# Causal windowed attention times a gated binary FFN: the products with v ahead of the scores in each step of the attention, k of the first sequence projected by halves, its v in PSUM of the attention

## The chip, the core and the metric

One Trainium2 chip, of which one core runs the kernel. The metric is the device time in microseconds (us); the median of three runs counts. A profile is taken of one execution of its own, whose time is given beside its span, the stretch that the records of the engines cover. Short names of the engines: PE is TensorE, DVE VectorE, ACT ScalarE, POOL GpSimd, SP SyncE (it issues DMAs). PEld is the loading of weights on PE.

## The reference

Eight sequences of 512 tokens with 256 channels. The normalised input goes into an attention of 16 heads of 16 channels with rotary positions, in which a token sees itself and the 249 before it, and into a network of three layers whose weights are +1 or -1; the attention's output times silu of the network's is added to the input.

```python
# x: [8, 512, 256]
xn = layernorm(x)
q, k, v = split(xn @ in_proj_w.T)          # 16 heads x 16
q, k = rotate(q), rotate(k)
mask = (delta >= 0) & (delta < 250)        # delta = pos_q - pos_k
attn = softmax(where(mask, q @ k.T / 4, lowest))
s = concat_heads(attn @ v) @ out_proj_w.T
h = s0 * (concat(xn, -xn) @ sign(k0))      # 512 -> 1024
h = s1 * (2 * relu(h) @ sign(k1))          # 1024 -> 1024
h = s2 * (2 * relu(h) @ sign(k2))          # 1024 -> 256
y = x + s * silu(h)
```

## The kernel before

**The order of work.** The body is a list of pieces, each with a place on an axis of planned time, a cost and a function. `run` (L226) sorts them by place and calls them one after another; its clock is the sum of the costs. A function issues its matmuls and may return followers, each with a delay; a follower is put out before the first piece at which the clock has passed its time. Each engine executes what it was given in this order, and waits for buffers and data by semaphores. So the places in `everything` (L966), in `prepare` (L446) and in `attention` (L827), and the delays, are the whole schedule. A sequence takes 42 units (`SEQ`, L213).

**What a sequence does.** For the first sequence x is transposed on PE (`turn_x`, L315); its parts for the network (a high part in fp16, a low part in fp32r) come from `first_parts` (L349), which is called for tiles 0 and 1 from the list and for 2 and 3 behind the last transpose. For the others the statistics go through DRAM and are applied to a transposed load (`stats` L245, `lay_down`, `lay_over`, `norm_turned`). `project` (L368) makes the parts a and b of k and of q, each in two matmuls of 128x512, multiplies them by cosine and sine on DVE (`times`), rotates on POOL (`rotate`), splits into high and low on ACT and DVE (`split_hi`, `split_lo`), writes both to DRAM and loads them stacked by groups of four heads (`stack`, L438). `project_v` (L354) makes v in four tiles of 128 tokens, which ACT copies into `v_pad`. The network's layers are in `layer` (L481): matmuls of the high, then of the low parts, a relu on ACT that writes the high part, and a subtraction on DVE that writes the low one. The third layer is `last` (L533).

**Attention.** A sequence's attention has nine steps (L682), spread over its 42 units between matmuls of the network. In a step (L819) `scores` (L701) issues the scores of up to 512 columns for four heads into two PSUM tiles; `exponentials` (L723) has ACT write them to p in two halves and POOL set to zero what the mask excludes (`mask`, L740); `values` (L767) multiplies p of the step before with v into `po`. A step thus issues its own scores, then the products of the step before (`flush`, L812), and hands out the exponentials of its own as followers. When a group's last products are issued, `keep` (L797) takes po out of PSUM: numerators V and sums S. S is inverted on DVE (`invert`, L861), V multiplied on POOL (`divide`, L865), and `project_o` (L887) projects and adds x.

**PSUM.** Three pools: `ps_s` two tiles of two banks (the two halves of a step's scores; at the start also two of the transposes and q of the first sequence), `ps_o` one tile (`po`, and the target of the warm-up matmuls, `warm`, L220), `ps_m` three tiles of one bank, which serve all else: h, v, k, q, z, the output's projection. A function that takes a tile waits until its last user has read it.

**The start.** Nine warm-up matmuls, two transposes, two more warm-ups, two transposes, one more warm-up, then k, q, the first layer with a tile of v after the second, fourth, sixth and eighth of its groups, and the second layer. Between them ACT and POOL make the weights of the second layer from bytes (`make_w1`, L188). A fallback for inputs with vanishing variance or huge scores (L1000 on) is compiled and doesn't run.

```python
0819  def step(b, i):
0820      sc, n = scores(b, i)
0821      had = len(pending)
0822      more = flush() or []
0823      p, masks, exps = exponentials(b, i, sc, n)
0824      pending.append((exps, masks, (b, i, p)))
0825      return [(-0.7 if had else 0.0, exps)] + more
```

Of the kernel before, what the change touches and what calls it, by code (L numbers as in the profile page):

```python
# [11 lines left out]
F32 = mybir.dt.float32  # L12
# [22 lines left out]
def tile_attention_times_gated_ffn(  # L35
# [42 lines left out]
    nc = tc.nc  # L78
    P = 128
    B, T, E = x.shape  # L80
    H = HEADS
# [233 lines left out]
    def turn_x(b, t, plain=False):  # L315

        st = states[b]
        xn = xs.pop((b, t))
        if t == 0:
            st["xT"] = one.tile([P, EC, T], F32, tag="xT", name=f"xT_{b}")  # L320
            if plain:
                st["xp"] = one.tile([P, EC, T], F32, tag="xl", name=f"xp_{b}")
            else:
                for p, dt in (("h", F16), ("l", F32R)):
                    st["x" + p] = one.tile([P, EC, T], dt, tag="x" + p, name=f"x{p}_{b}")
        if not plain and t < 2:

            pt = ps_s.tile([P, 2, T], F32, tag="sc", name=f"xnT_ps_{b}_{t}")
            pt = pt[:, 0, : EC * P].rearrange("p (c q) -> p c q", c=EC)
        else:  # L330
            pt = ps_m.tile([P, EC, P], F32, tag="mm", name=f"xnT_ps_{b}_{t}")
        for c in range(EC):
            nc.tensor.transpose(pt[:, c, :], xn[:, ts(c, P)], ident)
        if plain:
            nc.vector.tensor_copy(st["xT"][:, :, ts(t, P)], pt)
            nc.scalar.mul(st["xp"][:, :, ts(t, P)], pt, sgnx)
            return
        hi, lo = (st["x" + p][:, :, ts(t, P)] for p in "hl")


        nc.scalar.copy(st["xT"][:, :, ts(t, P)], pt)
        st["parts", t] = [
            lambda: nc.scalar.mul(hi, pt, sgnx),
            lambda: nc.vector.scalar_tensor_tensor(lo, pt, sgnx, hi, ALU.mult, ALU.subtract),
        ]
        if t + 1 == NT:
            first_parts(2, 3)

    def first_parts(*tiles):  # L349
        for t in tiles:  # L350
# [2 lines left out]

    def project_v(b, t):  # L354
        st = states[b]
        v = ps_m.tile([P, H // 2, 2, D], F32, tag="mm", name=f"v_ps_{b}_{t}")
        for c in range(EC):
            nc.tensor.matmul(  # L358
                v.rearrange("p n s d -> p (n s d)"),
                st["xT"][:, c, ts(t, P)],  # L360
                wqkv_sb[:, c, 2 * E :],
                start=(c == 0),
                stop=(c == EC - 1),
            )
        return [(0.0, lambda: nc.scalar.copy(v_pad[:, t, :, 0:3:2, :], v))]  # L365


    def project(b, what, part):  # L368
        st = states[b]
        col = E * "qk".index(what) + P * "ab".index(part)  # L370
        if b == 0 and what == "q":
            ps = ps_s.tile([P, 2, T], F32, tag="sc", name=f"{what}{part}_ps_{b}")[:, 0]
        else:
            ps = ps_m.tile([P, T], F32, tag="mm", name=f"{what}{part}_ps_{b}")
        for c in range(EC):
            nc.tensor.matmul(  # L376
                ps, wqkv_sb[:, c, ds(col, P)], st["xT"][:, c, :],
                start=(c == 0), stop=(c == EC - 1),
            )

        m = turned.tile(
            [P, 2, T], F32, tag=f"m{part}", name=f"m_{what}{part}_{b}",
# [1 line left out]
        )  # L384
        st[what, part] = m

        hi_after, lo_after = (4.0, 5.1) if b else (7, 8.2) if what == "k" else (6, 7.2)

        def times(i):
            nc.vector.tensor_tensor(  # L390
# [55 lines left out]
    def prepare(b, plain=False):  # L446

        if b == 0 or plain:
            at = dict(stats=-40, norm=-38, x=-36, k=0, q=3, v=9.2)
            dp, dv = 1.5, 1.5  # L450
        else:

            at = dict(load=9, stats=9, down=10.5, over=12, norm=16.8, k=21.8, q=24.8, v=SEQ + 0.6)
            if b == 1:
                at.update(load=18.65, stats=12, down=18.64, over=19.5, norm=23, k=27, q=29)
            dp, dv = 1.5, 1.0
            at = {n: SEQ * (b - 1) + f for n, f in at.items()}
        out = [(at["stats"], 0, lambda: stats(b))]
# [12 lines left out]
                ]  # L471
            out.append((at["v"] + dv * t, 0.87, lambda t=t: project_v(b, t)))
        for what in "kq":
            out += [
                (at[what], 1.75, lambda w=what: project(b, w, "a")),
                (at[what] + dp, 1.75, lambda w=what: project(b, w, "b")),
            ]
        return out


# [336 lines left out]
            return values(*of_step)  # L817

    def step(b, i):  # L819
        sc, n = scores(b, i)  # L820
        had = len(pending)
        more = flush() or []
        p, masks, exps = exponentials(b, i, sc, n)
        pending.append((exps, masks, (b, i, p)))
        return [(-0.7 if had else 0.0, exps)] + more

    def attention(b, among):  # L827
# [17 lines left out]
        for g in range(NG):  # L845

            at = times[used[g - 2][-1]] + 0.01 if g > 1 else first - (
                2.0 if b == 0 else 4.0 if b == 1 else 9.0
            )
            if b and g == 1:  # L850
                at = first + 0.01
# [3 lines left out]
        return out  # L855

    def ends_at(b):
        return SEQ * b + (30.0 if b + 1 == B else SEQ)


    def invert(b, pair, n):  # L861
# [76 lines left out]
    def divisions(b):  # L938
        out = []
        for pair in range(2):  # L940
            if b + 1 < B:
                first, d = (SEQ * b + 30.0, 2.0) if pair == 0 else (SEQ * (b + 1) + 4.2, 2.0)
            else:
                first, d = SEQ * b + (20.0 if pair == 0 else 30.6), 1.3
            for n in range(4):
                out.append((first + d * n, 0, lambda p=pair, n=n: invert(b, p, n)))
            out.append((first + d * 4, 0, lambda p=pair: divide(b, p)))
# [13 lines left out]
    def swap():  # L961
# [2 lines left out]
        outs = ctx.enter_context(tc.tile_pool(name="outs", bufs=1))  # L964

    everything = [  # L966
        (-34.6, 0, signs), (-40.5, 0, lambda: warm(9)), (-34.7, 0, lambda: warm(2)),
        (-32.5, 0, lambda: warm(1)), (-31.0, 0, lambda: enough(0)),
        (-32.7, 0, lambda: first_parts(0, 1)),
        (19.2, 0, make_w2), (22.5, 0, swap), (SEQ * (B - 1) + 45.0, 0, add_up),  # L970
    ]
    for c in range(EC):
        everything += [
# [153 lines left out]
```

## Time and profile before

| | us |
|---|---|
| runs (median of three) | 617.72 (617.2 to 617.77) |
| profiled execution | 617.83 |
| its span | 616.1 |
| PE busy | 598.1 |
| PE loading weights | 367.5 |
| DVE busy | 381.7 |
| POOL busy | 308.8 |
| ACT busy | 294.9 |

Mean granted clock of PE 0.995. By groups of the page, the network's matmuls (h_ps, L497) take 146.5 + 123.1 + 52.3 + 38.4, the products (L786) 77.3, the scores (L712) 57.5, z (L551) 35.8 and v (L358) 33.1 of PE's time. ACT spends 138.3 on 144 halves of exponentials; POOL 91.6 and 48.8 on masks, 722 and 509 ns each.

How to read the lines below. A line of the timeline has start, duration, engine, line and operation, output <- inputs, shape, the number of instructions joined, and in brackets the idle time before it with the engine, tile and line that ended it. PE's time busy is modelled, so a start-to-start difference tells the length of a block better than the durations. A line of the table of stretches has the stretch, its length, busy time and number of instructions of PE, PEld, DVE, ACT and POOL, the granted clock, the DMA engines' busy share and GB/s.

### The profile page before, as it was taken

The numbers are of one execution on the slowest core, as the hardware profiler recorded it, in microseconds if no ns is written. First come the engines' busy times: TensorE is split into PE (matmuls) and PEld (weight loads), VectorE is DVE, ScalarE is ACT, GpSimd is POOL, SyncE is SP. The second block draws the span as 40 slices with busy tenths as digits, with TensorE's granted clock in tenths as the row PEclk, the third lists the DMA queues.
The fourth block names the chain that finished last, engine by engine and source line by source line (L and its number), as shares of the span: only waits on it lengthen the run. The fifth ranks groups of instructions, "written<-read, shape, count | busy, mean of one in ns | idle before, by whom it ended". The sixth has DMA issues, their size and how long they took to land.

```text
span 616.1 us, 11176 instructions
## 1 busy us (share of the span) xinstructions
PE 598.1 (97%) x4490; PEld 367.5 (60%) x4490; DVE 381.7 (62%) x606; ACT 294.9 (48%) x414; POOL 308.8 (50%) x368
## 2 busy tenths in 40 slices
PE   8898999999999999999999999999999999999995
PEld 5453556556655566655565565655565556666794
DVE  7824545665765666655846658566576566655574
ACT  4555465345444355435455454544545435644421
POOL 2943551436723465236654466254672356626642
PEclk9998999999999999999999999999999999999998
DMA  8361370325342163222533153333524216212201
GB/s 275 152 239 53 120 271 20 112 113 194 95 138 89 70 230 113 87 86 109 199 103 121 51 203 106 111 119 115 195 87 141 91 70 224 85 52 70 81 8 40
DMA packets 38061, 74.51 MB, mean 121 GB/s; under 512 B 5360, under 2 KB 13040, under 8 KB 38000
## 3 DMA queue, kind: packets, MB, share of 16 engines
q1 hardware_dynamic: 35568, 71.48, 33.5%
q10 hardware_dynamic: 2432, 2.23, 1.1%
q8 instruction: 37, 0.61, 0.4%
q14 instruction: 24, 0.20, 0.1%
HBM read 44.30 MB, written 29.39 MB: 120 GB/s over the span
## 4 chain that ended last, share of the span: by engine, by line
PE 91%; DVE 4%; POOL 2%; DMA 1%; ACT 1%; issue 1%; SPq 0%; DVEq 0%; ACTq 0%; POOLq 0%
PE h_ps L497 44%; PE po L786 11%; PE z_ps L551 9%; PE sc L712 8%; PE v_ps L358 4%; PE att_ps L895 4%; PE ka_ps L376 3%; PE qb_ps L376 2%; PE qa_ps L376 2%; PE kb_ps L376 2%; PE warm L224 1%; DMA of_all<-d 1%; ACT p L731 1%; DMA d<-moments 1%; DVE den L568 1%
## 5 line engine op out<-in xcount | busy, mean ns | idle before, releaser
L731 ACT ACTIVATE p<-sc 128x1024 f32<-128x1024 f32 (+2 forms) x144 | 138.3, 1013 | 77.9 <-PE sc L712 43.8
L747 POOL TENSOR_SCALAR_AFFINE_SELECT p<-p 128x512 f32<-128x512 f32 x128 | 91.6, 722 | 136.2 <-ACT p L731 135.7
L497 PE MATMUL h_ps<-h1l,w1l_sb 128*128 128x512 f32 (+1 forms) x576 | 146.5, 396 | 0.0
L497 PE MATMUL h_ps<-h1h,w1h_sb 128*128 128x512 f16 (+1 forms) x576 | 123.1, 357 | 0.5 <-ACT v_pad L365 0.5
L497 PEld LDWEIGHTS h_ps<-h1l,w1l_sb 128*128 128x128 f32 x576 | 100.3, 188 | 29.6 <-issue 9.3
L508 ACT ACTIVATE h2h<-h_ps 128x512 f16<-128x512 f32 (+1 forms) x72 | 39.5, 548 | 115.8 <-PE h_ps L497 115.5
L497 PEld LDWEIGHTS <-w1h_sb 128*128 128x128 f16 x576 | 51.2, 98 | 59.0 <-issue 17.8
L754 POOL TENSOR_SCALAR_AFFINE_SELECT p<-p 128x512 f32<-128x512 f32 (+1 forms) x96 | 48.8, 509 | 74.6 <-ACT p L731 72.3
L786 PE MATMUL po<-p,v_pad 128*32 128x378 f32 (+4 forms) x1216 | 77.3, 373 | 3.1 <-DVE S L810 1.2
L612 DVE RECIPROCAL den<-den 128x256 f32<-128x256 f32 (+1 forms) x32 | 52.6, 1645 | 25.2 <-POOL den L607 25.2
L712 PEld LDWEIGHTS sc<-q,k 32*128 32x128 f32 x1216 | 44.1, 184 | 31.9 <-issue 20.6
L506 DVE SCALAR_TENSOR_TENSOR h2l<-h_ps,h2h 128x512 fp32r<-128x512 f32 (+1 forms) x72 | 43.9, 610 | 30.6 <-ACT h2h L508 30.5
L712 PE MATMUL sc<-q,k 32*128 32x378 f32 (+4 forms) x1216 | 57.5, 306 | 2.2 <-ACT p L731 2.2
L506 DVE SCALAR_TENSOR_TENSOR h1l<-h_ps,h1h 128x512 fp32r<-128x512 f32 x64 | 42.7, 679 | 24.7 <-ACT h1h L508 24.7
L863 DVE RECIPROCAL S<-S 128x128 f32<-128x128 f32 x64 | 57.4, 918 | 0.0
L497 PE MATMUL h_ps<-xl,w0l_sb 128*128 128x512 f32 x128 | 52.3, 489 | 0.0
L786 PEld LDWEIGHTS po<-p,v_pad 128*32 128x32 f32 x1216 | 31.7, 109 | 32.0 <-issue 17.7
L508 ACT ACTIVATE h1h<-h_ps 128x512 f16<-128x512 f32 x64 | 38.1, 598 | 21.5 <-PE h_ps L497 21.4
L301 DVE TENSOR_TENSOR xT<-xT,of_all 128x512 f32<-128x512 f32 x28 | 22.5, 805 | 32.2 <-DMA of_all<-d 31.8
L497 PE MATMUL h_ps<-xh,w0h_sb 128*128 128x512 f16 x128 | 38.4, 381 | 0.2 <-ACT v_pad L365 0.2
L551 PE MATMUL z_ps<-h2l,w2l_sb 128*128 128x512 f32 (+1 forms) x144 | 35.8, 390 | 0.0
L358 PE MATMUL v_ps<-wqkv_sb,xT 128*128 128x256 f32 x128 | 33.1, 381 | 2.0 <-DVE h1l L506 2.0
(101 smaller groups left out, 723.5 us busy)
## 6 DMA issues: line engine op xcount, KB each, us to landing
q<-dq SPq DMA_DIRECT2D x64, 256.0 KB, 3.5
dq<-qh SPq DMA_DIRECT2D x16, 512.0 KB, 3.3
dq<-m_qa SPq DMA_DIRECT2D x16, 512.0 KB, 5.3
k<-dk SPq DMA_DIRECT2D x32, 256.0 KB, 2.8
dk<-kh SPq DMA_DIRECT2D x8, 512.0 KB, 3.5
dk<-m_ka SPq DMA_DIRECT2D x8, 512.0 KB, 2.6
x<-in_x_dram SPq DMA_DIRECT2D x30, 128.0 KB, 2.8
xT<-in_x_t_dram SPq DMA_DIRECT2D x7, 512.0 KB, 5.2
```

Of the source, the lines that this page charges most:

```text
L358: nc.tensor.matmul(v.rearrange("p n s d -> p (n s d)"), st["xT"][:, c, ts(t, P)], wqkv_sb[:, c, 2 * E :], start=(c == 0), stop=(c == EC - 1),)
L376: nc.tensor.matmul(ps, wqkv_sb[:, c, ds(col, P)], st["xT"][:, c, :], start=(c == 0), stop=(c == EC - 1),)
L497: nc.tensor.matmul(ph, w[p][:, c, ts(f, P)], st[src + p][:, c, cols], start=(k == 0), stop=(k == n - 1),)
L506: nc.vector.scalar_tensor_tensor(lo, ph, 0.0, hi, ALU.max, ALU.subtract)
L508: high = lambda: nc.scalar.activation(hi, ph, AF.Relu)
L551: nc.tensor.matmul(pz, w2[p][:, c, ts(f, P)], st["h2" + p][:, c, cols], start=(c == 0 and p == "h"), stop=(c == NF1 - 1 and p == "l"),)
L612: nc.vector.reciprocal(part, part)
L712: nc.tensor.matmul(sc[r // 2][:, r % 2, ds(off, n)], st["k0", g][row, ts(j, P)], st[f"q{turn}", g][row, ds(j * P + first, n)], start=(turn ...
L731: nc.scalar.activation(p[:, 2 * half : 2 * half + 2, :n], sc[half][:, :, :n], AF.Exp, scale=D ** -0.5,)
L747: nc.gpsimd.affine_select(out=block, in_=block, compare_op=ALU.is_ge, fill=0.0, base=0, pattern=[[0, 4], [1, P]], channel_multiplier=-1,)
L786: nc.tensor.matmul(po[32 * r : 32 * r + 32, ds(j * P + first, n)], v_columns(j, g, r), p_[:, r, ds(off, n)], start=(j == 0), stop=(done an ...
L863: nc.vector.reciprocal(part, part)
```

## The change

- `step`: the products of the step before are issued first, the step's scores behind them. The exponentials still follow the scores.
- `project` gets `half`: of the first sequence's k, part a and part b, the first 256 columns are projected between and behind the transposes, the other 256 at the old place. The half's PSUM tile is kept until then. Three warm-up matmuls go (`warm(2)` and `warm(1)`; `warm(0)` issues none but still takes the tile).
- `turn_x`: the third transpose goes to `ps_o`, since the half of k takes a tile of `ps_m`. `first_parts` for tiles 0 and 1 comes behind the last transpose and for 2 and 3 from the list.
- `project_v`: v of the first sequence goes to `ps_s`.
- Delays and places: the splits of the first sequence's k and q sooner (4.5 and 5.7, 5 and 6.2, for 7 and 8.2, 6 and 7.2); the second sequence's statistics later and its load, k and q by some tenths of a unit; the first stacked loads 1.5 units sooner; the last sequence's steps over 33 units for 30, its divisions 2.5 and 3 later, the adding up of the counts 2.6 later.

```diff
--- before.py
+++ after.py
@@ -323,7 +323,10 @@
             else:
                 for p, dt in (("h", F16), ("l", F32R)):
                     st["x" + p] = one.tile([P, EC, T], dt, tag="x" + p, name=f"x{p}_{b}")
-        if not plain and t < 2:
+        if not plain and t == 2:
+            pt = ps_o.tile([P, T], F32, tag="po", name=f"xnT_ps_{b}_{t}")
+            pt = pt[:, : EC * P].rearrange("p (c q) -> p c q", c=EC)
+        elif not plain and t < 2:
 
             pt = ps_s.tile([P, 2, T], F32, tag="sc", name=f"xnT_ps_{b}_{t}")
             pt = pt[:, 0, : EC * P].rearrange("p (c q) -> p c q", c=EC)
@@ -344,7 +347,7 @@
             lambda: nc.vector.scalar_tensor_tensor(lo, pt, sgnx, hi, ALU.mult, ALU.subtract),
         ]
         if t + 1 == NT:
-            first_parts(2, 3)
+            first_parts(0, 1)
 
     def first_parts(*tiles):
         for t in tiles:
@@ -353,7 +356,11 @@
 
     def project_v(b, t):
         st = states[b]
-        v = ps_m.tile([P, H // 2, 2, D], F32, tag="mm", name=f"v_ps_{b}_{t}")
+        if b == 0:
+            v = ps_s.tile([P, 2, T], F32, tag="sc", name=f"v_ps_{b}_{t}")[:, 0, :E]
+            v = v.rearrange("p (n s d) -> p n s d", s=2, d=D)
+        else:
+            v = ps_m.tile([P, H // 2, 2, D], F32, tag="mm", name=f"v_ps_{b}_{t}")
         for c in range(EC):
             nc.tensor.matmul(
                 v.rearrange("p n s d -> p (n s d)"),
@@ -365,18 +372,25 @@
         return [(0.0, lambda: nc.scalar.copy(v_pad[:, t, :, 0:3:2, :], v))]
 
 
-    def project(b, what, part):
+    def project(b, what, part, half=None):
+
         st = states[b]
         col = E * "qk".index(what) + P * "ab".index(part)
         if b == 0 and what == "q":
             ps = ps_s.tile([P, 2, T], F32, tag="sc", name=f"{what}{part}_ps_{b}")[:, 0]
+        elif half == 1:
+            ps = st.pop(part)
         else:
             ps = ps_m.tile([P, T], F32, tag="mm", name=f"{what}{part}_ps_{b}")
-        for c in range(EC):
-            nc.tensor.matmul(
-                ps, wqkv_sb[:, c, ds(col, P)], st["xT"][:, c, :],
-                start=(c == 0), stop=(c == EC - 1),
-            )
+            st[part] = ps
+        for cols in [slice(0, T)] if half is None else [ts(half, T // 2)]:
+            for c in range(EC):
+                nc.tensor.matmul(
+                    ps[:, cols], wqkv_sb[:, c, ds(col, P)], st["xT"][:, c, cols],
+                    start=(c == 0), stop=(c == EC - 1),
+                )
+        if half == 0:
+            return
 
         m = turned.tile(
             [P, 2, T], F32, tag=f"m{part}", name=f"m_{what}{part}_{b}",
@@ -384,7 +398,7 @@
         )
         st[what, part] = m
 
-        hi_after, lo_after = (4.0, 5.1) if b else (7, 8.2) if what == "k" else (6, 7.2)
+        hi_after, lo_after = (4.0, 5.1) if b else (4.5, 5.7) if what == "k" else (5, 6.2)
 
         def times(i):
             nc.vector.tensor_tensor(
@@ -452,7 +466,7 @@
 
             at = dict(load=9, stats=9, down=10.5, over=12, norm=16.8, k=21.8, q=24.8, v=SEQ + 0.6)
             if b == 1:
-                at.update(load=18.65, stats=12, down=18.64, over=19.5, norm=23, k=27, q=29)
+                at.update(load=18.65, stats=15, down=18, over=18.7, norm=24.8, k=26.6, q=28.4)
             dp, dv = 1.5, 1.0
             at = {n: SEQ * (b - 1) + f for n, f in at.items()}
         out = [(at["stats"], 0, lambda: stats(b))]
@@ -471,10 +485,17 @@
                 ]
             out.append((at["v"] + dv * t, 0.87, lambda t=t: project_v(b, t)))
         for what in "kq":
-            out += [
-                (at[what], 1.75, lambda w=what: project(b, w, "a")),
-                (at[what] + dp, 1.75, lambda w=what: project(b, w, "b")),
-            ]
+            for n, part in enumerate("ab"):
+                if b == 0 and what == "k" and not plain:
+
+                    out += [
+                        (-34.3 if n == 0 else -32.95, 0.87, lambda p=part: project(b, "k", p, 0)),
+                        (at["k"] + dp * n, 0.87, lambda p=part: project(b, "k", p, 1)),
+                    ]
+                else:
+                    out.append((
+                        at[what] + dp * n, 1.75, lambda w=what, p=part: project(b, w, p),
+                    ))
         return out
 
 
@@ -817,9 +838,10 @@
             return values(*of_step)
 
     def step(b, i):
-        sc, n = scores(b, i)
+
         had = len(pending)
         more = flush() or []
+        sc, n = scores(b, i)
         p, masks, exps = exponentials(b, i, sc, n)
         pending.append((exps, masks, (b, i, p)))
         return [(-0.7 if had else 0.0, exps)] + more
@@ -845,7 +867,7 @@
         for g in range(NG):
 
             at = times[used[g - 2][-1]] + 0.01 if g > 1 else first - (
-                2.0 if b == 0 else 4.0 if b == 1 else 9.0
+                3.5 if b == 0 else 4.0 if b == 1 else 9.0
             )
             if b and g == 1:
                 at = first + 0.01
@@ -855,7 +877,7 @@
         return out
 
     def ends_at(b):
-        return SEQ * b + (30.0 if b + 1 == B else SEQ)
+        return SEQ * b + (33.0 if b + 1 == B else SEQ)
 
 
     def invert(b, pair, n):
@@ -941,7 +963,7 @@
             if b + 1 < B:
                 first, d = (SEQ * b + 30.0, 2.0) if pair == 0 else (SEQ * (b + 1) + 4.2, 2.0)
             else:
-                first, d = SEQ * b + (20.0 if pair == 0 else 30.6), 1.3
+                first, d = SEQ * b + (22.5 if pair == 0 else 33.6), 1.3
             for n in range(4):
                 out.append((first + d * n, 0, lambda p=pair, n=n: invert(b, p, n)))
             out.append((first + d * 4, 0, lambda p=pair: divide(b, p)))
@@ -964,10 +986,10 @@
         outs = ctx.enter_context(tc.tile_pool(name="outs", bufs=1))
 
     everything = [
-        (-34.6, 0, signs), (-40.5, 0, lambda: warm(9)), (-34.7, 0, lambda: warm(2)),
-        (-32.5, 0, lambda: warm(1)), (-31.0, 0, lambda: enough(0)),
-        (-32.7, 0, lambda: first_parts(0, 1)),
-        (19.2, 0, make_w2), (22.5, 0, swap), (SEQ * (B - 1) + 45.0, 0, add_up),
+        (-34.6, 0, signs), (-40.5, 0, lambda: warm(9)), (-34.7, 0, lambda: warm(0)),
+        (-31.0, 0, lambda: enough(0)),
+        (-32.7, 0, lambda: first_parts(2, 3)),
+        (19.2, 0, make_w2), (22.5, 0, swap), (SEQ * (B - 1) + 47.6, 0, add_up),
     ]
     for c in range(EC):
         everything += [
```

## The prediction

> **What bounds the kernel now.** I read the page's busy rows first, then the chain that ended last, then a table of stretches, then every place where TensorE (PE) waits.
>
> ```profile
> PE 598.1 (97%) x4490; PEld 367.5 (60%) x4490; DVE 381.7 (62%) x606; ACT 294.9 (48%) x414; POOL 308.8 (50%) x368
> PE 91%; DVE 4%; POOL 2%; DMA 1%; ACT 1%; issue 1%; SPq 0%; DVEq 0%; ACTq 0%; POOLq 0%
> ```
>
> PE holds 91% of the chain, so the change, which takes three tiny warm-up matmuls out and otherwise only reorders, can move the end through PE's idle time and clock alone. The table of stretches (length, then busy time of PE, PEld, DVE, ACT, POOL, granted clock, DMA share, GB/s) says where that idle time lies:
>
> ```profile
> 9.73:20.60 10.87, 10.87 (x35) 5.57 (x35) 8.19 (x16) 7.47 (x12) 5.92 (x5) 1.00 0.65 192
> 20.60:31.15 10.55, 7.91 (x33) 4.64 (x32) 10.34 (x20) 6.32 (x12) 10.55 (x9) 1.00 0.51 201
> 31.15:50.00 18.85, 17.22 (x114) 10.50 (x113) 5.85 (x14) 10.86 (x13) 7.31 (x7) 1.00 0.57 195
> 50.00:92.00 42.00, 39.61 (x357) 21.35 (x358) 19.09 (x28) 23.60 (x29) 22.91 (x31) 0.96 0.46 161
> 92.00:176.00 84.00, 84.00 (x611) 50.69 (x610) 51.76 (x80) 40.45 (x58) 39.78 (x49) 1.00 0.32 109
> 554.00:587.00 33.00, 31.75 (x353) 24.07 (x350) 17.97 (x28) 14.78 (x22) 22.00 (x26) 1.00 0.23 74
> ```
>
> The head and the first sequence hold nearly all of it; sequences 1 to 6 have none (84.00 of 84.00); one wait stands in the last sequence. In 20.60:31.15 POOL and DVE are full instead. The timeline of PE gives the waits by name:
>
> ```profile
> 29.56 1.13 PE L358 MATMUL v_ps<-wqkv_sb,xT 128*128 128x256 f32 x4 [1.43 <-DVE h1l L506]
> ...
> 31.15 1.89 PE L497 MATMUL h_ps<-h1h,w1h_sb 128*128 128x512 f16 x8 [0.46 <-ACT v_pad L365]
> ...
> 49.91 0.33 PE L712 MATMUL sc<-q,k 32*128 32x128 f32 x2 [1.63 <-ACT p L731]
> 50.80 0.84 PE L712 MATMUL sc<-q,k 32*128 32x128 f32 x14 [0.57 <-ACT p L731]
> ...
> 52.96 0.97 PE L786 MATMUL po<-p,v_pad 128*32 128x256 f32 x8 [0.60 <-POOL p L754]
> 53.86 3.30 PE L376 MATMUL ka_ps<-xT,wqkv_sb 128*128 128x512 f32 x4
> ...
> 79.60 0.43 PE L786 MATMUL po<-p,v_pad 128*32 128x128 f32 x8 [0.96 <-POOL p L747]
> ```
>
> The reader is to see three kinds: v of the first sequence waiting for a buffer that VectorE (DVE) must empty; scores waiting for the exponentials that empty theirs; products with v waiting for masks. The ka block at 53.86 starts after three waits and takes 3.30 where such a block otherwise takes about 1.8.
>
> **What the Trainium skill says.** "TensorE: Matmul & The Clock Gate", Part 1, "What's actually happening": the clock falls to half after an idle window of about 3.4 us, and windows run freely. The trace agrees: half clock from 53.3 to 56.8, 3.4 us, behind waits of 1.63 + 0.57 + 0.60. Whether new waits cost clock thus depends on where windows fall. "TensorEngine Tiling (Array Packing)", "Key Properties": a change of tiling mode drains TensorE. The trace shows it as last start to next start: 0.32 from an h block to scores, 0.20 from scores to products, 0.21 to 0.31 from products to h. The new order has as many such changes; products to scores is the one that before never shows. "SBUF — State Buffer", "SBUF: two separate sides": DVE and GpSimd (POOL) share a port pair that one of them locks; a low split takes 2.17 us beside a rotation at 22.04 and 1.21 alone, so moves on POOL and DVE near the head have uncertain durations.
>
> **The change, part by part.** Profiled execution 617.83 (span 616.1 and 1.73 around it), 0.11 above the median of 617.72; the sum is made against 617.83.
>
> *The head.* Half of ka and of kb goes between and behind the transposes, replacing three warm-up matmuls; the last projection ends near 15.95 instead of 16.70 (estimate). v of the first sequence moves to the attention's two score buffers, so h of layer 1 has all three others; the waits of 0.15, 0.41, 1.43 for DVE's h1l and 0.18, 0.46 for ScalarE's (ACT) copy of v go. What is late next: v_1 needs ACT's copy of v_0, and this stands behind the cast of k (1.04), which waits for POOL's rotation of k. In the timeline POOL reaches that behind kb1, landed at 14.49, and two blocks of w1l, so it stays where it is, 17.02 to 19.52. That puts v_1 near 21.65, h_4 at 22.75 (before 22.47), and from there four h groups of 0.91 and two v of 0.86 run through: 22.75 + 5.4 = 28.1 for layer 2, against 31.15. −3.05. Beyond it q must have landed: the first group's last load lands at 38.02, scores start at 38.43; with the splits earlier by as much I put both near 35.4. Bound: nothing gained (0), or −3.5.
>
> *The first sequence.* From its first scores at 38.43 to the next sequence's first h at 90.94 are 52.5 us. By start-to-start times against a quiet block, the waits cost 1.70 (h to sc2), 1.16 (within sc2), 1.10 (products of step 1), 1.40 (ka at half clock), 0.25 and 0.93 (products of step 6): 6.5. Scores now come behind the products of the previous step, so their buffers are long empty: the first two go. New waits, from ACT's 1.94 per pair of exponentials and POOL's 0.64 per mask: products of step 0 behind masks that stand behind two w1l blocks, 0.8 (0 to 1.4); of step 2, with only ka (1.8) between scores and products against 0.16 + 1.94 + 0.64 = 2.75 and the hand-over, 1.1; the first of group 1, 0.25; of step 5 behind the rotation of q (2.5), which waits for DVE's m_qb, 1.85 (1.0 to 2.1); of step 6, 0.8. Sum 4.8. These again may pull the clock down: half a chance of 1.3, +0.65. So −6.5 + 4.8 + 0.65 = −1.05 (bounds −3.5 and +1.5). Stats of the second sequence move behind h1l_7; low w1 and w2 on POOL wait for that, hidden behind layer 2 except in the 0.8 above.
>
> *Head and first sequence together*: −3.05 − 1.05 = −4.1.
>
> *Sequences 1 to 7.* PE is full and its amount of work equal, so the swap gains nothing. It delays the exponentials of most steps by the products now in front (0.36 to 1.0 of a block). Within sequences the next products come 4 us or more later and the cover holds (closest: step 6, mask ready about 0.5 before it is needed). At a sequence's start it doesn't:
>
> ```profile
> 308.97 0.79 PE L712 MATMUL sc<-q,k 32*128 32x378 f32 x16
> 309.69 1.05 PE L786 MATMUL po<-p,v_pad 128*32 128x244 f32 x16
> 309.85 1.94 ACT L731 ACTIVATE p<-sc 128x1024 f32<-128x1024 f32 x2 [0.18 <-PE sc L712]
> 311.58 1.02 PE L358 MATMUL v_ps<-wqkv_sb,xT 128*128 128x256 f32 x4
> 311.78 0.60 ACT L508 ACTIVATE h1h<-h_ps 128x512 f16<-128x512 f32 x1
> 312.64 0.37 ACT L365 COPY v_pad<-v_ps 128x256 f32<-128x256 f32 x1 [0.27 <-PE v_ps L358]
> 313.34 1.02 PE L358 MATMUL v_ps<-wqkv_sb,xT 128*128 128x256 f32 x4
> ```
>
> ACT runs two exponentials, h1h of the first layer, then the copy of v_0, whose buffer the second v takes at 313.34. With scores behind products the exponentials start 1.0 later: 310.85 + 1.94 + 0.60 + 0.37 = 313.76 against 313.34: PE waits 0.4, I take 0.38, for each of seven sequences, +2.65. Below: nothing, if ACT's copy is early or the loss is made up; above: v_2 and v_3 pay again. Queued behind v_1 on PE is h_2 and all after it, so there is nothing to absorb it.
>
> *The last sequence.* Its steps spread over 33 instead of 30 of the planner's units. The wait of 1.25 for S before the products at 566.33 shrinks to about 0.35; against it the sum of the counts and its cast move behind the last gate, +0.3 on DVE, and z's last quarter finds DVE up to 0.7 later. Net −0.3 (−1.2 to +0.5).
>
> Sum: 617.83 − 4.1 + 2.65 − 0.3 = 616.1, less 0.11 for the median: 616.0.
>
> **The rivals.** *B, the sequences' starts are free.* The 0.38 is a difference of two chains, and the copy could run before the exponentials end if ACT's order or the hand-over is kinder; for it: every later sequence is full in before; against it: ACT's first exponential had only 0.18 idle before it. Time: 617.83 − 4.1 − 0.3 − 0.11 = 613.3.
>
> *C, slower.* At each sequence's start ACT, late by one products block, doesn't catch up: v_1, v_2 and v_3 each wait 0.38, 1.14 a sequence, 8.0 for seven. 617.83 − 4.1 + 8.0 − 0.3 − 0.11 = 621.3. It decides from (4.1 + 0.3) / 7 = 0.63 us a sequence. For it: ACT's copies of v have only 0.27 idle before them. Against it: between v_1 and v_2 ACT has 0.97 of work in 1.77.
>
> *D, given back.* The change does what it says to the named waits, but the first sequence ends no earlier than the head gives: two slow-clock windows, masks behind rotations at their upper bounds, q landing late. The gain is 2.6 instead of 4.1; 617.83 − 2.6 + 2.65 − 0.3 − 0.11 = 617.5, no change.
>
> **How the numbers follow.** Forecast 0.48, own range 614.5 to 617.3; B 0.20; D 0.18; C 0.14. A measurement of this kernel can tell 0.2%, 1.24 us: faster is below 616.5, slower above 619.0. Faster: two thirds of the forecast, 0.32, B's 0.20, and 0.02 of D: 0.54. Same: 0.16 of the forecast, 0.13 of D, 0.01 of C: 0.30. Slower: 0.13 of C, 0.03 of D: 0.16. For 8 in 10 the range reaches B's time with its half microsecond below, 612.6, and past D to the lower end of C, 618.8.
>
> **What would show it.** Right: no wait of v for h1l in the head; layer 2 at 28 to 28.5; no wait of sc for p in the first sequence, but waits of po for masks of some 4 to 5 us there; the second sequence's first h at 86 to 87.5; seven waits of v_ps for v_pad of about 0.4, and PE full elsewhere. Wrong: layer 2 or the first scores held by q's loads, waits in the middle of sequences 1 to 6, or starts of sequences without a wait, or with three.

## The result, and the profile after

The changed kernel takes 618.36 us (median of 14 runs, 617.34 to 619.98) where the kernel before, run beside it, takes 617.46 (14 runs, 615.44 to 620.19). The ratio is 1.0009, with an interval from 0.9996 to 1.0023: no change that can be measured. The profiled execution took 618.13, its span 616.4.

Four marks of PE's timeline divide the two executions: the end of the first scores (start of the matmul behind them), the first h of the second sequence, the first h of the eighth, and the start of the last projection's last matmul.

| us | before | after | difference of the stretch |
|---|---|---|---|
| first scores done | 39.15 | 37.66 | -1.49 |
| second sequence's first h | 90.94 | 88.11 | -1.34 |
| eighth sequence's first h | 530.41 | 529.63 | +2.05 (six laps, 73.24 to 73.59) |
| last matmul of the projection | 608.64 | 608.71 | +0.84 |
| end of the span | 616.1 | 616.4 | +0.24 |

So the 2.8 us that are won up to the second sequence are given back by the rest. The page's busy row and the table of stretches of the changed kernel (length, busy time of PE, PEld, DVE, ACT, POOL, clock, DMA share, GB/s):

```profile
PE 596.2 (97%) x4492; PEld 365.6 (59%) x4492; DVE 384.5 (62%) x606; ACT 291.8 (47%) x414; POOL 313.9 (51%) x368
```

```profile
20.60:31.15 10.55, 7.99 (x36) 5.11 (x37) 9.03 (x14) 7.72 (x14) 9.91 (x7) 1.00 0.58 226
31.15:50.00 18.85, 18.17 (x140) 10.87 (x139) 12.36 (x25) 12.35 (x16) 11.28 (x11) 1.00 0.53 182
50.00:92.00 42.00, 38.02 (x336) 21.26 (x335) 18.82 (x26) 23.01 (x29) 22.44 (x31) 1.00 0.49 163
92.00:176.00 84.00, 83.93 (x608) 50.16 (x607) 51.92 (x80) 39.22 (x56) 39.05 (x47) 1.00 0.32 107
554.00:587.00 33.00, 32.00 (x359) 25.23 (x348) 19.20 (x31) 14.66 (x22) 21.87 (x26) 1.00 0.23 74
```

PE is busy for less of 50 to 92 than before, and yet the first sequence is done sooner, partly because the clock is full there (1.00 for 0.96). And 83.93 of 84.00 is the first sign that the later sequences are no longer full. PE's waits in the timeline of the changed kernel, but for those of the first 9 us:

```profile
22.10 1.13 PE L365 MATMUL v_ps<-wqkv_sb,xT 128*128 128x256 f32 x4 [1.80 <-ACT v_pad L372]
24.29 0.59 PE L518 MATMUL h_ps<-xh,w0h_sb 128*128 128x512 f16 x2 [1.06 <-DVE h1l L527]
41.95 1.07 PE L807 MATMUL po<-p,v_pad 128*32 128x378 f32 x16 [0.55 <-POOL p L775]
52.32 0.43 PE L807 MATMUL po<-p,v_pad 128*32 128x128 f32 x8 [0.94 <-POOL p L768]
70.02 1.50 PE L807 MATMUL po<-p,v_pad 128*32 128x378 f32 x24 [1.89 <-POOL p L775]
75.45 1.01 PE L807 MATMUL po<-p,v_pad 128*32 128x244 f32 x16 [1.04 <-POOL p L775]
566.83 1.50 PE L807 MATMUL po<-p,v_pad 128*32 128x378 f32 x24 [1.00 <-DVE S L831]
603.10 0.38 PE L572 MATMUL z_ps<-h2l,w2l_sb 128*128 128x256 f32 x1 [0.20 <-DVE h2l L527]
```

No score waits for exponentials any more; products wait for masks instead.

### The profile page after: what moved, and what is told of

The parts are those of the page before. It is cut to its first block, busy times and chain, and to the rows that moved or that the text cites. A ratio compares the mean times of both kernels' runs of the same rounds, so it can differ in the third digit from the quotient of the medians.

```text
span 616.4 us, 11147 instructions
## 1 busy us (share of the span) xinstructions
PE 596.2 (97%) x4492; PEld 365.6 (59%) x4492; DVE 384.5 (62%) x606; ACT 291.8 (47%) x414; POOL 313.9 (51%) x368
## 5 line engine op out<-in xcount | busy, mean ns | idle before, releaser
L768 POOL TENSOR_SCALAR_AFFINE_SELECT p<-p 128x512 f32<-128x512 f32 x128 | 95.1, 750 | 130.4 <-ACT p L752 129.3
L529 ACT ACTIVATE h1h<-h_ps 128x512 f16<-128x512 f32 x64 | 37.3, 601 | 14.3 <-PE h_ps L518 14.2
```

The source lines that it names most:

```text
L529: high = lambda: nc.scalar.activation(hi, ph, AF.Relu)
L768: nc.gpsimd.affine_select(out=block, in_=block, compare_op=ALU.is_ge, fill=0.0, base=0, pattern=[[0, 4], [1, P]], channel_multiplier=-1,)
```

## The experiments

All marks are of the profiled execution of each kernel, the times of its timed runs; the ratio is to the kernel before on the same chip, with its 95% interval. "First" is the second sequence's first h minus the end of the first scores, "lap" the mean of the six stretches from one sequence's first h to the next one's, up to the eighth, and "last" goes from the eighth's first h to the start of the last projection's last matmul. A name that starts with ns_ is no_swap (the changed kernel with the scores first again) with one more part undone.

| kernel | first scores done | first | lap | last | median us (runs) | ratio |
|---|---|---|---|---|---|---|
| before | 39.15 | 51.79 | 73.24 | 78.24 | 617.46 (14) | |
| changed | 37.66 | 50.45 | 73.59 | 79.08 | 618.36 (14) | 1.0009 (0.9996 to 1.0023) |
| s0_scores_first | 37.03 | 50.96 | 73.26 | 78.73 | 615.83 (11) | 0.9966 (0.9951 to 0.9981) |
| half1_late | 37.34 | 50.38 | 73.24 | 78.74 | 617.42 (16) | 0.9987 (0.9972 to 1.0001) |
| no_swap | 37.29 | 46.73 | 73.25 | 77.50 | 610.45 (5) | 0.9879 (0.9856 to 0.9901) |
| swap_alone | 40.78 | 55.36 | 73.59 | 82.02 | 625.27 (5) | 1.0113 (1.0089 to 1.0137) |
| ns_second_old | 38.60 | 52.92 | 73.25 | 77.49 | 617.04 (12) | 0.9982 (0.9966 to 0.9997) |
| ns_v_ps_m | 41.30 | 46.01 | 73.24 | 77.49 | 612.87 (4) | 0.9911 (0.9880 to 0.9941) |
| ns_k_whole | 37.59 | 47.21 | 73.24 | 77.49 | 612.29 (5) | 0.9921 (0.9892 to 0.9949) |
| ns_last_old | 37.73 | 46.52 | 73.25 | 78.24 | 611.03 (4) | 0.9908 (0.9885 to 0.9931) |
| second_alone | 42.05 | 48.30 | 73.24 | 78.24 | 617.97 (20) | 1.0009 (0.9997 to 1.0022) |
| second_and_loads | 38.61 | 45.74 | 73.24 | 78.22 | 612.41 (6) | 0.9924 (0.9905 to 0.9943) |
| best1 | 36.30 | 46.03 | 73.25 | 77.80 | 609.47 (5) | 0.9862 (0.9838 to 0.9886) |
| best2 | 35.39 | 46.22 | 73.24 | 77.26 | 607.98 (4) | 0.9858 (0.9835 to 0.9881) |

**What the start of a sequence costs.** The theory was the prediction's: the second v waits for ScalarE's copy of the first behind later exponentials. The timeline of the changed kernel at the third sequence:

```profile
161.01 0.80 PE L733 MATMUL sc<-q,k 32*128 32x378 f32 x16
...
161.89 1.94 ACT L752 ACTIVATE p<-sc 128x1024 f32<-128x1024 f32 x2 [1.16 <-PE sc L733]
...
162.65 1.02 PE L365 MATMUL v_ps<-wqkv_sb,xT 128*128 128x256 f32 x4
...
163.72 0.60 ACT L529 ACTIVATE h1h<-h_ps 128x512 f16<-128x512 f32 x1
...
164.19 0.39 ACT L372 COPY v_pad<-v_ps 128x256 f32<-128x256 f32 x1
...
164.64 0.73 PEld L365 LDWEIGHTS v_ps<-wqkv_sb,xT 128*128 128x128 f32 x4 [0.50 <-ACT v_pad L372]
```

Behind the first v the next h starts at 163.51, but ScalarE copies that v only at 164.19, behind h1h, and the load of weights for the second v shows the wait. It isn't in the PE rows, whose modelled ends overlap; one sees it in start-to-start times (0.89 from the h block at 163.75 to this v at 164.64, where 0.66 is usual; the v itself then takes 0.97 for 0.86) and in PEld. Together that is the 0.34 by which a lap grew. Two kernels attack this cause in different ways. In s0_scores_first only the first step of later sequences has the scores first:

```diff
+        first = b > 0 and i == 0
+        if first:
+            sc, n = scores(b, i)
         more = flush() or []
-        sc, n = scores(b, i)
+        if not first:
+            sc, n = scores(b, i)
```

> The changed kernel, but in the first step of the second to eighth sequence the scores stand ahead of the products again, as before; all other steps keep the new order. Theory A (the lap of a sequence, from its first h matmul to that of the next, grew from 73.25 to 73.58 us because the second v of a sequence waits for the copy of the first one behind later exponentials): laps of 73.25 again, the first h of the eighth sequence at about 527.3 instead of 529.6, and the end about 2.3 us sooner, near 616.1 by the clock of the changed kernel's 618.4. Theory B (the loss is spread over all nine steps, as tile changes from products to scores cost more): laps of 73.54 or more, no gain to speak of (at most 0.3 us).

In half1_late PE's order is untouched; the second half of the exponentials of a sequence's first step is handed out later:

```diff
-            return [(0.3, second)]
+            return [(2.5 if b and i == 0 else 0.3, second)]
```

> The changed kernel, PE's order untouched; in the first step of the second to eighth sequence the second half of the exponentials goes behind the copy of the first v on ScalarE instead of ahead of the first h1h. Theory A: the second v finds its buffer free, laps of 73.25, the end about 2.3 us sooner (near 616.1), unless the third v or the fourth h now waits behind the moved half (up to 0.3 a lap, then no gain). Theory B (PE's own order of tiles costs it): laps stay at 73.58, because PE's order is that of the changed kernel.

Both have laps of 73.24 to 73.26. The timeline of half1_late shows the copy ahead of the second exponential:

```profile
307.62 1.03 ACT L752 ACTIVATE p<-sc 128x1024 f32<-128x1024 f32 x1 [1.16 <-PE sc L733]
...
308.58 0.60 ACT L529 ACTIVATE h1h<-h_ps 128x512 f16<-128x512 f32 x1
...
309.44 0.37 ACT L372 COPY v_pad<-v_ps 128x256 f32<-128x256 f32 x1 [0.27 <-PE v_ps L365]
...
309.71 1.03 ACT L752 ACTIVATE p<-sc 128x1024 f32<-128x1024 f32 x1
...
310.14 1.02 PE L365 MATMUL v_ps<-wqkv_sb,xT 128*128 128x256 f32 x4
```

That settles it: eight other steps of the new order cost a later sequence nothing, the first one 0.34. By the clock s0_scores_first is faster than before; half1_late's interval touches 1, with runs from 614.77 to 619.09, and its lap is the evidence.

**What the order of a step is worth.** no_swap puts the scores first again in every step and keeps all else of the change; swap_alone makes the swap in the kernel before and nothing else.

> The changed kernel with the scores ahead of the products in every step, as before; k by halves, v in the attention's PSUM, the delays and the last sequence's places stay. Theory A: laps 73.25; the head is that of the changed kernel (second layer at about 29.6, first scores at about 36.9); in the first sequence the waits of scores for exponentials return, so from the first scores to the second sequence's first h some 52.5 us instead of 51.2, which puts that h at about 89.4 instead of 88.1. The end some 1 us sooner than the changed kernel: laps -2.3, first sequence +1.3. Rival: the first sequence needs only 51.2 in this order too, since its gain came from the other moves of the change; then that h at 88.1 and the end 2.3 us sooner.

> The kernel before, with nothing but the products ahead of the scores in every step. Theory A: head as before (second layer at about 31.1, first scores at 38.4), laps of 73.58 in place of 73.25 (+2.4 us in all), and the first sequence 1.3 us shorter (51.2 from its first scores to the next sequence's first h): the end about 1 us later than the kernel before. Rival: the swap is neutral in the first sequence, because waits of products for masks take the place of waits of scores for exponentials; then +2.4 us.

Both theories missed by far. Without the swap the change is 1.2% faster than before; the swap alone is 1.1% slower. The first sequence didn't lose 1.3 without it, it won 3.7 (46.73 for 50.45, both at full clock). With the swap alone it became 3.6 longer (55.36 for 51.79), but that profiled execution, 629.19, is the longest of its runs, and its clock from 50 to 92 is 0.88 where before has 0.96: by an estimate from these (42 x 0.08) some 3.4 of the 3.6 are clock, so the 3.7 is the cleaner size.

The scores' waits for exponentials, which I had taken to be removed by the swap, are gone from no_swap too, but for 0.20. In swap_alone they are gone by name only. Its timeline:

```profile
48.84 0.72 ACT L307 ACTIVATE xh<-xT,sgnx 128x512 f16<-128x512 f32 x1 [3.99 <-DVE xT L301]
...
49.94 1.89 ACT L731 ACTIVATE p<-sc 128x1000 f32<-128x1000 f32 x2
...
52.82 1.04 PE L786 MATMUL po<-p,v_pad 128*32 128x244 f32 x8 [2.30 <-POOL p L754]
```

ScalarE still takes the second sequence's x ahead of step 1's exponentials, and where the scores of before waited 1.63 and 0.57 for those, the products now wait 2.30 for the masks behind them. How the swap makes products late elsewhere shows in the chain to the products of step 5, first in the changed kernel:

```profile
59.84 1.94 ACT L752 ACTIVATE p<-sc 128x1024 f32<-128x1024 f32 x2 [3.18 <-PE sc L733]
61.67 1.05 ACT L442 CAST kh<-m_ka 128x1024 fp32r<-128x1024 f32 x1
...
62.75 1.66 DVE L449 TENSOR_TENSOR m_ka<-m_ka,kh 128x1024 fp32r<-128x1024 f32 x1 [6.04 <-ACT kh L442]
...
65.52 1.27 DVE L404 TENSOR_TENSOR m_qb<-qb_ps,rope_sb 128x512 f32<-128x512 f32 x2
...
66.28 2.50 POOL L425 TENSOR_TENSOR m_qa<-m_qa,m_qb 128x512 f32<-128x512 f32 x2 [1.79 <-DVE m_qb L404]
...
69.33 0.64 POOL L775 TENSOR_SCALAR_AFFINE_SELECT p<-p 128x512 f32<-128x512 f32 x1
```

and in no_swap:

```profile
57.06 1.94 ACT L752 ACTIVATE p<-sc 128x1024 f32<-128x1024 f32 x2 [2.54 <-PE po L807]
58.89 1.05 ACT L442 CAST kh<-m_ka 128x1024 fp32r<-128x1024 f32 x1
...
62.73 1.27 DVE L404 TENSOR_TENSOR m_qb<-qb_ps,rope_sb 128x512 f32<-128x512 f32 x2
...
63.49 2.52 POOL L425 TENSOR_TENSOR m_qa<-m_qa,m_qb 128x512 f32<-128x512 f32 x2 [1.79 <-DVE m_qb L404]
...
66.56 0.64 POOL L775 TENSOR_SCALAR_AFFINE_SELECT p<-p 128x512 f32<-128x512 f32 x1
...
67.68 1.50 PE L807 MATMUL po<-p,v_pad 128*32 128x378 f32 x24
```

Against the projection of q (starts at 61.16 and at 59.52) the exponentials of step 4 come 1.32 earlier in the changed kernel and 2.46 earlier without the swap: 1.14 later, as the products of step 3 stand ahead of their scores. On ScalarE the cast of k is queued behind them, on VectorE the low split and q's multiplication, on POOL the rotation, and behind that the mask for which the products at 70.02 wait. At the other end PE comes to the products 0.83 sooner (the length of a block of scores, 71.45 to 72.28), because the scores no longer stand ahead. A step's products lose cover, that is, time in which PE has other work, at both ends: their exponentials start later by the block of products in front of the scores, and they are due sooner by the block of scores that stood in front of them.

**What the rest of the change is worth.** From no_swap, one part after the other was undone. The places of the second sequence:

```diff
-                at.update(load=18.65, stats=15, down=18, over=18.7, norm=24.8, k=26.6, q=28.4)
+                at.update(load=18.65, stats=12, down=18.64, over=19.5, norm=23, k=27, q=29)
```

> The changed kernel with the scores first again, and with the second sequence's statistics, load, normalisation, k and q at the places that they had before. Theory C: before's waits of scores for exponentials in the first sequence (1.63 + 0.57 us) came from ScalarE, which stood at the high part of the second sequence's x, behind the DMA of its statistics, ahead of the exponentials of step 1; the change took them away by moving those places, not by the order in a step. Then they are back here: 2 us or more of waits of scores and of products behind them near 46 to 52 us, the second sequence's first h at 86 to 90 us instead of 84.0, the end 2 to 6 us later than with scores first alone (610.4). Rival (the waits went because the head is 3 us sooner, or because statistics come earlier): that h at 84.0 to 84.6, the end within 0.6.

The waits of before are back to the hundredth, as PE's timeline of ns_second_old shows:

```profile
49.34 0.33 PE L733 MATMUL sc<-q,k 32*128 32x128 f32 x2 [1.63 <-ACT p L752]
50.23 0.84 PE L733 MATMUL sc<-q,k 32*128 32x128 f32 x14 [0.57 <-ACT p L752]
```

"First" is 52.92 for 46.73, of which an estimated 3.4 is clock (0.92 from 50 to 92 for 1.00). In ns_second_old ScalarE takes the second sequence's x at 47.19, ahead of step 1's exponentials at 48.29. In no_swap it is the other way round:

```profile
41.74 1.90 ACT L752 ACTIVATE p<-sc 128x1000 f32<-128x1000 f32 x2
...
46.24 0.72 ACT L307 ACTIVATE xh<-xT,sgnx 128x512 f16<-128x512 f32 x1 [2.60 <-DVE xT L301]
```

So it was ScalarE standing at the second sequence's x, ahead of step 1's exponentials. The head isn't it: ns_last_old, whose second layer starts at 29.71 as against 29.48 here, still needs 46.52. Then v in the pool of the h:

```diff
-        if b == 0:
+        if b < 0:
             v = ps_s.tile([P, 2, T], F32, tag="sc", name=f"v_ps_{b}_{t}")[:, 0, :E]
```

> The changed kernel with the scores first again, and v of the first sequence in the pool of the h again. If the attention's PSUM is what took the waits of v for h1l out of the head, they are back (1 to 2.5 us), the second layer starts at 29.3 to 30.7 instead of 28.2, and the second sequence's first h comes at 84.5 to 86 (1.0 of it is covered, since the first scores wait that long for q anyway). Rival: the wait of v for ScalarE's copy (1.3) merely changes its name, and the second layer starts within 0.3 of 28.2.

The first scores come 4.0 later than in no_swap, more than expected: waits of 2.21 and 1.14 stand beside a clock of 0.69 in 20 to 31. And k whole:

```diff
-                if b == 0 and what == "k" and not plain:
+                if False:
```

> The changed kernel with the scores first again, and k of the first sequence projected whole behind the transposes (the three warm-up matmuls stay out). If the halves help only PE, whose head is then held by POOL's rotation behind the bytes of the second layer's weights, the second layer starts within 0.3 of 28.2 and the end is the same within 0.5. Rival (k is 0.7 us later through the whole head, its multiplication on DVE and the rotation too): the second layer at 28.8 or later, the first scores wait longer for q, the end 0.7 us later or more.

0.3 at the first scores and 0.5 in the first sequence, where scores now wait for q's loads (0.54 and 0.23). That is nearer the rival, but the 0.3 isn't shown to be k's: ns_last_old, with k by halves, has its first scores at 37.73, later than the 37.59 here. By the clock the intervals of ns_k_whole and no_swap overlap. The last sequence's places (30 units, 20.0 and 30.6, 45.0) again:

> The changed kernel with the scores first again, and with the last sequence's steps, divisions and adding up at the places of before (30 units). Before had a wait of 1.25 us of products for S there and 78.24 us from the last sequence's first h to the last projection's last matmul; with the new places and the scores first these are 0 and 77.5. If the new places did that: the wait is back, 78.0 to 78.6, the sum of the counts is out of DVE's last chain (-0.3 there), and the end is 0.3 to 0.8 us later than with scores first alone. Rival: the wait is also gone with the old places, and the end is 0.3 us sooner.

78.24, the figure of before, with products waiting 1.24 for S: the new places take that wait away, and only with the scores first; with the swap 1.00 of it is back. The gain that was to come from the counts with the old places isn't seen: from the last matmul's start to the end 7.69, against 7.65 in no_swap.

**Is one part alone the gain?** second_alone has only the second sequence's places in the kernel before.

> The kernel before, with nothing changed but the places of the second sequence's statistics, load, normalisation, k and q (those of the change). Theory C (these places took the waits of scores for exponentials away): from the first scores to the second sequence's first h 46 to 49 us instead of 52.5, so that this h comes at 84.5 to 87.5 instead of 90.9, laps 73.25, and the end 3.5 to 6.5 us sooner than the kernel before. Rival (the places help only behind the new head, since here POOL's masks and the loads of q stand elsewhere): less than 2 us.

No gain by the clock, and yet no wait for exponentials. The timeline of second_alone says why, SyncE's queue first:

```profile
34.97 1.33 SPq L281 DMA_DIRECT2D d<-moments  x4
36.34 0.35 SPq L443 DMA_DIRECT2D k<-dk  x1
36.79 0.85 SPq L443 DMA_DIRECT2D q<-dq  x2
```

```profile
39.79 0.45 PE L712 MATMUL sc<-q,k 32*128 32x378 f32 x4 [2.72 <-DMA q<-dq]
41.10 1.01 PE L712 MATMUL sc<-q,k 32*128 32x378 f32 x12 [0.86 <-DMA q<-dq]
42.05 3.59 PE L497 MATMUL h_ps<-h1h,w1h_sb 128*128 128x512 f16 x8
```

The DMA of the statistics waits for VectorE and holds the loads of k and q behind it; in before they were issued from 31.56 on, ahead of it. Behind the wait the clock falls to half: the h block at 42.05 takes 3.03 start to start where 1.55 is usual. The change also issues the first stacked loads 1.5 units sooner, and with this one number added:

```diff
-                2.0 if b == 0 else 4.0 if b == 1 else 9.0
+                3.5 if b == 0 else 4.0 if b == 1 else 9.0
```

> The kernel before with the places of the second sequence's statistics, load, normalisation, k and q, and with the first stacked loads 1.5 units sooner, which puts them ahead of the DMA of the statistics on SyncE's queue. Theory D (the places alone gained nothing because that DMA, issued at 34.97 us, stood ahead of the loads of q, so that the first scores waited 2.72 + 0.86 for q and the clock fell to half behind it): here no wait of scores for q over 0.5 us, no half clock, the second layer near 29.7, the second sequence's first h at 84 to 86 instead of 90.35, the end 4.5 to 6 us sooner than before. Rival (q's low split, not the queue, sets q's landing): the wait of 2 us or more stays, and the gain is below 2 us.

Theory D holds: a wait of 0.47 for q, full clock, that h at 84.35, ratio 0.9924. These places and the loads are most of what the change has to give; the rest of it without the swap (v in the attention's PSUM, the halves, the delays, the last sequence's places) brings it to no_swap's 0.9879. Undone one by one, the parts cost 7.5 (second sequence), 3.3 (v) and 0.8 (k) at the second sequence's first h, against 6.9 that they win together: they overlap, and their single shares are not settled. Executions with the same first sequence differ by 0.2 at this mark (no_swap and ns_last_old).

**A kernel that beats both.** best1 adds to no_swap an order for POOL in which rotations stand ahead of weights, and later or sooner splits; best2 mends what best1 showed. What best2 has in place of no_swap's lines:

```diff
-        ("l", 0, -20, nc.gpsimd), ("l", 1, -19, nc.gpsimd), ("l", 2, 5.1, nc.gpsimd),
-        ("h", 0, -17, nc.scalar), ("h", 1, -16, nc.scalar), ("h", 2, 5.2, nc.gpsimd),
+        ("l", 0, 5.05, nc.gpsimd), ("l", 1, 11.5, nc.gpsimd), ("l", 2, 11.6, nc.gpsimd),
+        ("h", 0, -17, nc.scalar), ("h", 1, -16, nc.scalar), ("h", 2, 11.7, nc.gpsimd),
...
-        hi_after, lo_after = (4.0, 5.1) if b else (4.5, 5.7) if what == "k" else (5, 6.2)
+        hi_after, lo_after = (4.0, 5.1) if b else (4.5, 9.2) if what == "k" else (5.0, 7.4)
```

In its last sequence the test of S on POOL and the count behind it come later (2.6 and 2.6 for 0 and 1.5), the second gate sooner (10.2 for 11.0). best1 differs in q's splits (4.2 and 5.6 for 5.0 and 7.4) and in the count (1.2 for 2.6).

> A kernel that is to beat both: the changed one with the scores first again; POOL rotates k and q ahead of all but one block of the second layer's weights; the low split of the first k behind four h1l, that of q sooner; in the last sequence the gate of the second quarter ahead of the test of S on POOL. Against scores first alone (610.4): the wait of v for ScalarE's copy (1.3) and of the first scores for q (1.0) go, which is 1.5 to 2.3 us; the last quarter of z no longer waits for DVE (0.5). Expected near 608, the second layer at about 27, the second sequence's first h at about 82.0. Rival: the split of k stands in the way of an h (up to 1 us), or the weights that were put off are late for the second layer; then 609.5 or more.

> The kernel that was to beat both, once more: the high split of q behind the fifth h1h instead of ahead, its low split behind the sixth h1l, and in the last sequence the count behind the last h2l. Against its first form (608.0 of span): the two waits of h for h1l (0.76 and 0.75 us) and that of z (0.24 to 0.5) go, so 1.5 to 2 us sooner, a span near 606.3, unless q is late for the first scores (then 0.5 to 1 of it stays).

best1 lost 1.5 to h waiting for h1l (0.76 and 0.75), and 609.47 is the rival's figure; best2 has neither that wait nor z's, its layer 2 starts at 26.40, and behind it only 0.70 for q and 0.20 for exponentials are left; its span is 606.5, near the 606.3 expected. 607.98 is 1.4% under the kernel before. That best2 beats no_swap rests on the profile, since their intervals overlap.

## Why the prediction was right or wrong

The range held the time, and "same", to which the prediction gave 0.30, came out; the outcome that it held likelier, "faster" at 0.54 with 616.0, did not. That the time fell in the range is in part luck: the sum put the profiled execution at 616.1 where 618.13 came, and the range reached so far because it was drawn to take in rival D. Term by term:

- **The head, -3.05, was -1.5.** The step that failed is "from there four h groups of 0.91 and two v of 0.86 run through". In this execution h_4 waited 1.06 for h1l behind the low split of k, and the v ahead of it came at 22.10 instead of 21.65. In half1_late and no_swap, whose first 28 us hold the same instructions in the same order, the wait for h1l is missing and layer 2 starts at 28.24, close to the predicted 28.1. But then the first scores wait 0.77 to 0.80 for q: "I put both near 35.4" was the second miss, q landed near 36.7, so that even the better head ends its first scores at 37.3.
- **The first sequence, -1.05, was -1.3, with a wrong cause.** The new waits were put at 4.8; they are 0.55 + 0.94 + 1.89 + 1.04, and 0.34 in the block at 47.30, together 4.76, nearly all where the prediction named them: this half was right. No half clock came, where +0.65 stood. The gain of 6.5 is about right as a size (6.1 by these numbers), but its cause is not "scores now come behind the products of the previous step, so their buffers are long empty: the first two go". With the swap alone the same lateness comes back as a wait of products of 2.30, and no_swap is rid of it with the scores first. The second sequence's places took it away. The swap was credited with a gain that it doesn't make; its true cost there, 3.7, was hidden in the sum.
- **Starts of sequences, +2.65, were +2.05** for six laps and about 0.34 more in the last: right in place, mechanism and near in size, and shown by two kernels that undo it.
- **The last sequence, -0.3, was +0.84** to the last matmul. 0.34 is the second v. The wait for S shrank to 1.00, not to 0.35; with the scores first it is 0. The last quarter of z lost 0.55 to VectorE, about as bounded. These make 0.64; the other 0.2 isn't placed. The reduce and the cast stand in VectorE's last chain as said; the end came 0.24 later there.

Rival D, no change at 617.5, is near the time that came. Its gain of 2.6 ahead of the later sequences is near the 2.8 measured, but its mechanism isn't the one that came: it had the first sequence give nothing, by slow clock and late q, while here the clock was full, the first sequence gave 1.3, and the head gave half of what was forecast. B is refuted by the laps; C's second and third wait don't exist (the third v starts without one).

The profile of before did show who was late:

```profile
47.76 0.72 ACT L307 ACTIVATE xh<-xT,sgnx 128x512 f16<-128x512 f32 x1 [4.54 <-DVE xT L301]
...
48.86 1.89 ACT L731 ACTIVATE p<-sc 128x1000 f32<-128x1000 f32 x2
```

ScalarE's row at 47.76, the x of the second sequence, with 4.54 of idle time ahead of it, stands in front of the exponentials at 48.86 that the scores wait for. The prediction read the wait and its releaser, and not what stood ahead of the releaser on its own queue. Two smaller readings are off as well: the half clock of before stands from 53.1 to 56.5, not from 53.3 to 56.8 (its length, 3.4, is right), and the low split of 1.21 at 29.43 wasn't alone, since a block of POOL's began beside it at 29.85.

## What to carry to other kernels

Swapping two blocks on the bound engine took cover from both ends of the loop between them here: the consumer was due sooner by one block (0.83) and its producers started later by the other (1.14). Where the slack on the side engines was smaller than that sum, the swap cost time, and where the bound engine was full, in the later sequences, it won nothing. When a wait names an engine, look at what that engine did before the work that was late, and at which edit moves that. When pieces are moved on an engine's DMA queue, look at everything that then stands ahead of a load: here one number, 1.5 units, decided between no gain and 0.8%.

## What the hardware showed

One program has two heads. VectorE's low split of k and POOL's block of weights start within 0.1 us of each other. In the changed kernel's execution POOL gets through and VectorE pays:

```profile
21.45 2.19 DVE L449 TENSOR_TENSOR m_ka<-m_ka,kh 128x1024 fp32r<-128x1024 f32 x1
...
21.36 1.21 POOL L194 TENSOR_SCALAR w1h_sb<-kb,sgn,sgnn 128x1024 f16<-128x1024 uint8 x1
```

In no_swap's execution it is the other way round:

```profile
21.04 1.22 DVE L449 TENSOR_TENSOR m_ka<-m_ka,kh 128x1024 fp32r<-128x1024 f32 x1
...
20.96 2.28 POOL L194 TENSOR_SCALAR w1h_sb<-kb,sgn,sgnn 128x1024 f16<-128x1024 uint8 x1
```

The loser takes nearly its own time and the other's (2.19 and 2.28, where the winner takes 1.21 and 1.22). That fits what the Trainium skill ("SBUF — State Buffer", "SBUF: two separate sides") states, an exclusive lock for the whole instruction, held by the one that starts first. Who that is can't be read from the records: in both executions POOL's starts 0.08 or 0.09 ahead. It changed between executions of the same order, with layer 2 at 28.24 and 28.25 (no_swap, half1_late) where VectorE won, and at 29.01 to 29.71 (s0_scores_first, changed, ns_last_old) where POOL did. Part of the spread of the runs may come from it, which wasn't tried.

The change from products to scores, which before never had, takes 0.20 to 0.31 from last start to next start, no more than the change from products to h that it replaces (also 0.20 to 0.31).
